# Cross-attention rows of a decoder layer: the maximum added in the visit of the scores, masked places written from a broadcast tile

## The chip, the cores and the metric

The kernel runs on one core of one Trainium2 chip. The metric is device time in microseconds (us) of one execution. Five engines work side by side, each through its own instructions in order: TensorE (PE; its weight loads are listed as PEld), VectorE (DVE), ScalarE (ACT), GpSimd (POOL) and SyncE (SP), which here issues nearly all DMAs. They wait for one another by semaphores. PE writes its products to PSUM, eight banks of 2 KB per partition; DVE and ACT read them there; GpSimd works on SBUF alone.

## The reference, cut to what matters

One decoder layer with pre-normalisation, for 128 sequences of 128 tokens and width 256, in f32, with 16 heads of 16:

```python
x = x + self_attention(layernorm(x))
x = x + cross_attention(layernorm(x), ctx, ctx, mask)
x = x + ffn(layernorm(x))        # 256 -> 1024, exact gelu, layernorm, -> 256, ternary weights

# inside the cross attention:
scores = einsum('bhqd,bhkd->bhqk', Q, K) / sqrt(16)
scores = where(mask == 0, 1e-09, scores)       # one mask for all sequences and heads
attn = softmax(scores)
```

A masked place is not left out of the softmax: its score is 1e-09, and it gets the weight exp(1e-09 - max).

## The kernel before, in words

**Groups, rows and streams.** The 128 sequences are 32 groups of 4 (`G`). A group's tokens are 512 columns. What a group needs is written as Python generators that yield between pieces: `n` (load x, normalise, transpose, self queries, keys and values), `k` (load the context, cross keys and values), `c` (self projection, normalise, cross queries), `f` (cross projection, normalise, FFN, store), and `A`, the attention itself, which runs over all groups. Three strings, START, ORDER and END, name the stream that takes the next step, letter by letter (line 860). They are the order of the program: nothing reorders it afterwards. ORDER is repeated 28 times, and each repeat carries one group of every stream. So every engine's instruction order is fixed by these strings, and a piece of PE work between two attention steps is what covers DVE's and ACT's share of an attention row.

**An attention row** is one sequence with 16 heads, 128 x 128 scores each. `attention()` (line 822) walks through rows, four self rows of one group and four cross rows of the group before. For a row `here` with its neighbours `following` and `before`, it takes these steps:

- `maxima(following)` (line 680): PE computes scores with queries on partitions into all four score banks (two tiles of two banks, `ps_s`). In a cross row, sixteen small matmuls (L689, `never`) first put -1e30 at masked places. DVE takes maxima with two reductions (L711), negated, into `negm`; in a cross row `least` keeps them below the masked score (L717).
- `outputs(before)` (line 797): PE multiplies weights with values (L806), ACT copies the result to `raw` (L809); the values carry a column of ones, so the sums of weights come along.
- `transposed_scores(here)` (line 752): PE computes scores again, with keys on partitions (L761), into the same four banks. In a self row the queries already hold the maximum, added by `q_max` (L733). In a cross row DVE then writes the constant 1e-09 to masked places, with a predicated copy (L771) whose source is one column, `masked_score`.
- `transposed_maxima(following)` (line 725): PE turns `negm` over (L728). In a cross row ACT and DVE split it into three bf16 parts (L743 to L749), `negm_t`.
- `weights(here)` (line 778): in a cross row sixteen bf16 matmuls (L785) add the parts to the scores, masked places too, and ACT takes the exponentials (L794), one instruction for each pair of banks.

Thus a cross row uses its score banks from the scores through masking, additions and exponentials, and PE visits them twice. In the strings a cross row takes five letters A and a self row four. The stationary operand of the additions is `add_max`, a bf16 tile of 4 x 128 columns with equal columns for each of the four:

```python
rows = ident_strips[:, :, n:12:4]
nc.vector.tensor_reduce(row_of[:, n : n + 1], rows, AX.XY, ALU.add)
nc.vector.tensor_copy(add_max[:, n], row_of[:, n : n + 1].to_broadcast([P, P]))
```

**Keys and raw outputs.** `keys_values` (line 349) keeps a unit's keys in one tile of 512 columns, in two versions by the parity of the head; each is written by one ACT instruction of 512 columns (L358) for each half of the width, and three such tiles exist. `outputs` fills a `raw` tile of 512 columns over four rows. After the fourth, `rearranged` (line 385) issues two DMAs for the sums (L390) and eight for the outputs (L396), SBUF to SBUF. `projected` (line 399) takes reciprocals (L402), stores them to DRAM (L405), loads them back spread over partitions as `factors` (L408), and GpSimd multiplies (L414) before the output projection (L336, `po`).

**Other rows that the steps below use.** `transposed` (line 290) normalises with DVE's statistics (L275, L276), GpSimd's rstd (L281, L282) and its subtraction and product (L286). `hidden` (line 434) and `second` (line 469) are the FFN: products `ph` (L443) with Gelu (L450), normalisation on DVE or GpSimd (L286), transposes `pg` (L477), a split in two parts on ACT (L486) and DVE (L488), and products `py` (L501). `split` (L431, L432) does the like for the FFN's input. ACT loads a table for Gelu (L438) and one for Exp (L452). Three banks (`ps_mm`) serve all products but the attention's, one bank (`ps_av`) serves outputs and turned maxima. The last group is finished by `finish_rows` (line 608) in pieces x, y and z.

Of the kernel before, what the change touches and what calls it, by code (L numbers as in the profile page):

```python
# [53 lines left out]
    "nnnnnnwnwnnnwnnnAnAAnnAwnAAnAnAnAAAAAnnAAknnwAnnnnwnccnkAnnAAnnAnAkAcccckcAAcAnAAkccAccccntAAkAAnkAn"  # L54
    "AnAAnAkckAnnAnAcAnAnAnntAnAAAckccAccckkAAknAkAnknAnckcnAcAActAAftkAAAncAcAAntAAAffffAffnAnfnAnnAAnAn"
    "kAffnAAkfcfAffkfAAfknncffAAffffAkkfAnfcAcnfAfAffAAccfAc"
)
ORDER = (
    "ncfAfffAAkkAccAAcfcAnnfAAAccAffAAnnkAAnnAnfAnkAAAfffAfffnAAkcnnAnnAnAfkfkcAffffffAAfffAfffAfccccfffA"
    "fkfkAAAncfAn"  # L60
)
END = (
    "cfAfAffAfAcAcffcAfAAckAAxcAkcfffAAfffAAkfAAAAAkffkAcfAcAfffffAffAffccfffAcckcfckfAffAfAkkAfcAcfAAffc"
    "cAcfcAfAfkAAffAkAkfkAAAAfAfAffffAAxxAffAxAfffAxfffyfAfffffyfxAyffffAfxyxxxzxyfxfffzffyxzzffxxxxyyzxx"
    "yyzzzyzzz"
# [4 lines left out]
def tile_decoder_layer(ctx: ExitStack, tc: tile.TileContext, a: dict, out: bass.AP):  # L70
# [118 lines left out]
    for stage in ("self", "cross"):  # L189
        negms[stage] = const.tile([P, S4, 8, 4], F32, name=f"negm_{stage}")  # L190
# [10 lines left out]
    add_max = const.tile([P, 4, P], BF16, name="add_max")  # L201
# [39 lines left out]
    def constants():  # L241
# [15 lines left out]
        for n in range(4):  # L257
            rows = ident_strips[:, :, n:12:4]
            nc.vector.tensor_reduce(row_of[:, n : n + 1], rows, AX.XY, ALU.add)
            nc.vector.tensor_copy(add_max[:, n], row_of[:, n : n + 1].to_broadcast([P, P]))  # L260
        for i in range(2):
            rows = ident_strips[:, :, 4 * (i + 1) : 12]
# [86 lines left out]
    def keys_values(w, src_t, unit):  # L349
# [3 lines left out]
        for o in range(CC):  # L353
            pk = yield from product_halves(w["k"], o, src_t, "pk")
            if o == 0:
                kt = unit["k"] = p_act.tile([P, CC, 2, T], F32, name="kt", tag="kt", bufs=3)
            for e in range(2):
                nc.scalar.activation(  # L358
                    kt[:, o, e],
                    pk,  # L360
                    AF.Identity,
                    bias=w["bk"][:, o, e : e + 1],
                    scale=parity[:, e : e + 1],
                )
# [20 lines left out]
    def rearranged(raw):  # L385


        sums = p_stat.tile([P, T // 8], F32, name="sums", tag="sums", bufs=2)
        for o in range(CC):
            nc.sync.dma_start(sums[o * 64 : (o + 1) * 64], raw[HD :: P // S4, 2 * o : 2 * o + 2])  # L390
        o_raw = p_act.tile([P, CC, T], F32, name="o_raw", tag="o_raw")
# [514 lines left out]
```

## Time and profile before

| what | value |
|---|---|
| three executions | 2736.03, 2736.43 and 2738.77 us, median 2736.43 |
| profiled execution | span 2733.8 us from first to last instruction; 2.6 us less than the median |
| distance of two repeats of ORDER | 82.87 us |
| busy in one repeat | PE 82.51, DVE 65.18, ACT 49.21, POOL 41.76 us |
| bytes moved | 130.28 MB, mean 48 GB/s |
| q1, the queue that SyncE feeds | 125.11 MB, 19.0% of 16 DMA engines |

The page's time of the profiled execution is its span. A row of its groups reads: line, engine, operation, output tile and input tiles, shapes and count, then busy us, mean ns of one, and the engine's idle time before such instructions with what ended it. In a timeline the columns are start us, duration us, engine, line and operation, tiles, count, and in brackets the idle time before it. Ends of matmuls are modelled, so a busy PE can hide small gaps.

### The profile page before, as it was taken

To read this page: it belongs to the slowest core of one execution; us is meant where nothing else is said; L and a number is where in the kernel's file an instruction comes from. 1 tells how busy PE (TensorE), PEld (TensorE's weight loads), DVE (VectorE), ACT (ScalarE), POOL (GpSimd) and SP (SyncE) were. 2 spreads that over 40 slices of the span, in tenths; PEclk is the share of its full clock that TensorE was granted. 3 is DMA by queue.
4 is the path that set the end of the run, shared out by engine and by line. 5 is a ranking of instruction groups with operands and counts; after the bars stand their busy time and mean duration, and the time that the engine had idled before them with its cause. 6 is when DMAs were issued, how large, how long until landed. Compare 5 with 4: busy or idle time off the path is not lost.

```text
span 2733.8 us, 77048 instructions
## 1 busy us (share of the span) xinstructions
PE 2676.2 (98%) x32845; PEld 1917.3 (70%) x32845; DVE 2118.7 (78%) x3916; ACT 1579.2 (58%) x2508; POOL 1337.1 (49%) x1425
## 2 busy tenths in 40 slices
PE   7999999999999999999999999999999999999998
PEld 4567777677777767776777776777777777777666
DVE  5677787777787777887777887777877778877777
ACT  3455666655665655665556666556656556665446
POOL 3344554544554554554445545445545445545443
PEclk9999999999999999999999999999999999999999
DMA  4121111221111221122211112211112211212210
GB/s 118 33 50 42 41 41 50 57 57 34 46 44 50 57 58 28 46 49 51 58 42 41 42 50 57 58 42 42 42 49 58 58 31 44 49 49 50 50 26 16
DMA packets 110093, 130.28 MB, mean 48 GB/s; under 512 B 32312, under 2 KB 69048, under 8 KB 109752
## 3 DMA queue, kind: packets, MB, share of 16 engines
q1 hardware_dynamic: 109464, 125.11, 19.0%
q8 instruction: 259, 4.24, 0.6%
q14 instruction: 82, 0.67, 0.1%
q10 hardware_dynamic: 288, 0.26, 0.0%
HBM read 71.38 MB, written 18.84 MB: 33 GB/s over the span
## 4 chain that ended last, share of the span: by engine, by line
PE 89%; DVE 7%; issue 2%; POOL 1%; ACT 1%; DMA 0%; ACTq 0%; DVEq 0%; SPq 0%; POOLq 0%
PE st L761 10%; PE av L806 9%; PE pq L324 9%; PE s L700 9%; PE ph L443 9%; PE py L501 8%; PE pk L324 8%; PE po L336 8%; PE pv L336 8%; PE pt L304 3%; PE pg L477 2%; PE s L689 2%; PE st L785 2%; DVE mx L711 1%; DVE g L488 1%
## 5 line engine op out<-in xcount | busy, mean ns | idle before, releaser
L711 DVE TENSOR_REDUCE mx<-s 128x8 f32<-128x1024 f32 x512 | 601.3, 1216 | 83.0 <-PE s L700 82.5
L794 ACT ACTIVATE w_t<-st 128x1024 f32<-128x1024 f32 x512 | 496.7, 1022 | 202.5 <-PE st L785 122.3
L281 POOL TENSOR_SCALAR rstd<-agg 128x4 f32<-128x4 f32 (+2 forms) x163 | 39.0, 239 | 965.5 <-DVE agg L276 965.5
L286 POOL TENSOR_SCALAR xn<-x,agg,rstd 128x256 f32<-128x256 f32 x378 | 458.4, 1226 | 9.9
L771 DVE COPY_PREDICATED_SCALAR st<-masked_t,masked_score 128x1024 f32 x256 | 316.1, 1280 | 68.1 <-PE st L761 68.1
L414 POOL TENSOR_TENSOR o_raw<-o_raw,factors 128x256 f32<-128x256 f32 x252 | 181.0, 745 | 382.9 <-DMA factors<-by_head 277.0
L809 ACT COPY raw<-av 128x512 f32<-128x512 f32 x256 | 151.0, 590 | 315.3 <-PE av L806 310.4
L486 ACT ACTIVATE g<-pg,ln_w 128x256 fp32r<-128x256 f32 (+1 forms) x520 | 205.8, 473 | 175.8 <-PE pg L477 163.6
L700 PE MATMUL s<-kt,qt 32*128 32x256 f32 x4096 | 298.8, 402 | 3.2 <-ACT w_t L794 2.2
L501 PE MATMUL py<-w_proj,g 128*128 128x256 f32 x2048 | 279.6, 289 | 1.3 <-DVE g L488 0.8
L806 PE MATMUL av<-w_t,v 128*32 128x128 f32 x8192 | 276.9, 276 | 0.5 <-DVE q_max L733 0.5
L806 PEld LDWEIGHTS av<-w_t,v 128*32 128x32 f32 x8192 | 209.0, 109 | 96.7 <-issue 80.0
L443 PE MATMUL ph<-w_fc,xn 128*128 128x512 f32 x1024 | 259.8, 404 | 4.2 <-ACT g L450 1.6
L501 PEld LDWEIGHTS py<-w_proj,g 128*128 128x128 f32 x2048 | 254.1, 189 | 13.2 <-issue 1.3
L286 POOL TENSOR_SCALAR g<-g,agg,rstd 128x1024 f32<-128x1024 f32 x63 | 241.1, 3828 | 6.6
L488 DVE SCALAR_TENSOR_TENSOR g<-pg,ln_w,g 128x256 fp32r<-128x256 f32 (+1 forms) x520 | 212.6, 469 | 30.3 <-ACT g L486 29.9
L700 PEld LDWEIGHTS s<-kt,qt 32*128 32x128 f32 x4096 | 187.8, 185 | 63.7 <-issue 40.2
L443 PEld LDWEIGHTS ph<-w_fc,xn 128*128 128x128 f32 x1024 | 184.8, 188 | 58.7 <-DVE xn L432 10.0
L761 PEld LDWEIGHTS st<-q_max,kt 32*128 32x128 f32 x4096 | 129.2, 186 | 61.1 <-DVE negm_self L722 42.5
L275 DVE BATCH_NORM_STATS2 stats<-g 128x6 f32<-128x512 f32 x256 | 160.9, 670 | 0.8 <-ACT g L450 0.8
L450 ACT ACTIVATE g<-ph 128x512 f32<-128x512 f32 x256 | 146.5, 599 | 25.3 <-PE ph L443 24.2
L761 PEld LDWEIGHTS st<-qt,kt 32*128 32x128 f32 x4096 | 128.1, 186 | 46.3 <-DVE mx L711 26.4
(130 smaller groups left out, 4612.8 us busy)
## 6 DMA issues: line engine op xcount, KB each, us to landing
o_raw<-raw SPq DMA_DIRECT2D x504, 64.0 KB
factors<-by_head SPq DMA_DIRECT2D x126, 256.0 KB
ctx_t<-in_ctx_t_dram SPq DMA_DIRECT2D x32, 512.0 KB
x<-in_x_dram SPq DMA_DIRECT2D x31, 512.0 KB
out_dram<-x SPq DMA_DIRECT2D x31, 512.0 KB
sums<-raw SPq DMA_DIRECT2D x126, 16.0 KB
by_head<-r SPq DMA_DIRECT2D x63, 32.0 KB
raw_w<-in_w_fc_t_dram SPq DMA_DIRECT2D x1, 1024.0 KB
```

Of the source, the lines that this page charges most:

```text
L286: engine.tensor_scalar(dst[:, j], src[:, j], agg[:, j, 0:1], rstd[:, j : j + 1], ALU.subtract, ALU.mult)
L324: nc.tensor.matmul(out, w[:, c, o * P : (o + 1) * P], src_t[:, c], start=(c == 0), stop=(c == CC - 1))
L336: nc.tensor.matmul(rows[:, j], src_t[:, c, (j0 + j) * P : (j0 + j + 1) * P], w[:, c], start=(c == 0), stop=(c == CC - 1),)
L443: nc.tensor.matmul(ph, xn_parts[i][:, c, (j0 + j - at) * P : (j0 + j - at + 1) * P], w_fc[:, c, n * 512 : (n + 1) * 512], start=((i, c) == ...
L488: nc.vector.scalar_tensor_tensor(parts[1][:, f0 + f, tok], pieces[:, f], scales[f], parts[0][:, f0 + f, tok].bitcast(F32), ALU.mult, ALU.s ...
L501: nc.tensor.matmul(rows[:, j], parts[i][:, f, j * P : (j + 1) * P], w_proj[:, f], start=((i, f) == terms[0]), stop=((i, f) == terms[-1]),)
L700: nc.tensor.matmul(s[r // 2][:, r % 2, 2 * o : 2 * o + 2], qt[strip, o, tok], kt[strip, o, :, tok], start=(stage == "self"), stop=True, sk ...
L711: nc.vector.tensor_reduce(mx[:, 2 * half : 2 * half + 2], s[half], AX.X, ALU.max, negate=True)
L761: nc.tensor.matmul(s[r // 2][:, r % 2, n], kt[strip, n // 2, n % 2, tok], added[strip, n // 2, n % 2] if stage == "self" else qt[strip, n ...
L771: nc.vector.copy_predicated(s[half].rearrange("p r n q -> p (r n) q"), masked_t[:, None, :].to_broadcast([P, 8, P]), masked_score[:, :, No ...
L794: nc.scalar.activation(w_t[:, 2 * half : 2 * half + 2], s[half], AF.Exp)
L806: nc.tensor.matmul(av[32 * r : 32 * r + 32, n], v[:, j, head : head + 32], w_t[:, r, n], start=True, stop=True)
```

## The change

- **Additions first.** In a cross row the additions of the maximum now stand ahead of the scores, in one visit of PE in `transposed_scores`. `weights` is gone, and the predicated copy and the exponential follow pair of banks by pair of banks.
- **Masked places** are written last, so their value is 1e-09 - max, and differs by query and head. ACT writes the turned maxima plus 1e-09 to `m_rows`; one DMA stores 16 rows of it in DRAM (`by_row`, 8 KB), another loads them on all 128 partitions (`masked_as`, 1 MB, a single buffer). The predicated copy reads this tile.
- **Order of steps.** `transposed_maxima` of a following cross row comes before `transposed_scores` of the present row, and the load of `masked_as` is issued after it. A cross row takes four letters A. START, ORDER and END are new strings: 179, 108 and 269 letters for 255, 112 and 209.
- **Weights of the additions**: `add_max` has one column for each of the four, read 128 times by a step of 0. `negm` of cross rows lays out its parts the other way round.
- **Half tiles.** Keys are two tiles of 256 columns (five in all, for three of 512), each written by twice as many ACT instructions of 256 columns. `raw` is a tile of two rows (three buffers), and ten DMAs follow each half. The reciprocals go to DRAM in two DMAs.

Line numbers of the changed kernel differ by a few from those above.

```diff
 ORDER = (
-    "ncfAfffAAkkAccAAcfcAnnfAAAccAffAAnnkAAnnAnfAnkAAAfffAfffnAAkcnnAnnAnAfkfkcAffffffAAfffAfffAfccccfffA"
-    "fkfkAAAncfAn"
+    "AfffAnkAnnAfnAcnnnnnAnffAnfAfAfnnnfcffAAfffkAffffkAccccfffkAffkAAfAcfffAfknfkAcAAfAfAAkncfAcfAccAAAn"
+    "cckAAffA"
 )
...
-    add_max = const.tile([P, 4, P], BF16, name="add_max")
+    add_max = const.tile([P, 4], BF16, name="add_max")
...
-                kt = unit["k"] = p_act.tile([P, CC, 2, T], F32, name="kt", tag="kt", bufs=3)
-            for e in range(2):
-                nc.scalar.activation(
-                    kt[:, o, e],
-                    pk,
-                    AF.Identity,
-                    bias=w["bk"][:, o, e : e + 1],
-                    scale=parity[:, e : e + 1],
-                )
+                kt = unit["k"] = [
+                    p_act.tile([P, CC, 2, T // 2], F32, name="kt", tag="kt", bufs=5) for _ in range(2)
+                ]
+            for half in range(2):
+                for e in range(2):
+                    nc.scalar.activation(
+                        kt[half][:, o, e],
+                        pk[:, half * T // 2 : (half + 1) * T // 2],
+                        AF.Identity,
+                        bias=w["bk"][:, o, e : e + 1],
+                        scale=parity[:, e : e + 1],
+                    )
...
-    def rearranged(raw):
+    def rearranged(raw, half, sums, o_raw):
...
         for o in range(CC):
-            nc.sync.dma_start(sums[o * 64 : (o + 1) * 64], raw[HD :: P // S4, 2 * o : 2 * o + 2])
+            at = half * 64 + o * 32
+            nc.sync.dma_start(sums[at : at + 32], raw[HD :: P // S4, 2 * o : 2 * o + 2])
...
-                dst = o_raw[s * 32 + e * HD : s * 32 + (e + 1) * HD]
+                dst = o_raw[s * 32 + e * HD : s * 32 + (e + 1) * HD, :, half * T // 2 : (half + 1) * T // 2]
                 nc.sync.dma_start(dst, pairs[s * 32 : s * 32 + HD, e])
...
-        nc.sync.dma_start(by_head.rearrange("o h (j t) -> (o h j) t", j=8), r)
+        for half in range(2):
+            dst = by_head[:, :, half * T // 2 : (half + 1) * T // 2].rearrange("o h (j t) -> (o h) j t", j=4)
+            nc.sync.dma_start(dst, r[half * 64 : (half + 1) * 64])
...
+        rows = p_att.tile([P, P], F32, name="m_rows", tag="m_rows", bufs=1)
+        nc.scalar.activation(rows, pn, AF.Identity, bias=masked_score)
+        by_row = p_dram.tile([H, P], F32, name="by_row", tag="by_row")
+        nc.sync.dma_start(by_row, rows[0::8])
         first = p_att.tile([P, P], BF16, name="first", tag="first", bufs=1)
...
+    def masked_scores(by_row):
+        masked = p_att.tile([P, H, P], F32, name="masked_as", tag="masked_as", bufs=1)
+        nc.sync.dma_start(masked, by_row[None].to_broadcast([P, H, P]))
+        return masked
...
         if stage == "cross":
+            negm_t, masked = added
             for n in range(4):
                 for r in range(S4):
                     strip = slice(r * 32, (r + 1) * 32)
                     nc.tensor.matmul(
                         s[r // 2][:, r % 2, n],
-                        add_max[strip, n],
-                        added[strip],
-                        start=False,
-                        stop=(n == 3),
+                        add_max[strip, n : n + 1].to_broadcast([32, P]),
+                        negm_t[strip],
+                        start=(n == 0),
+                        stop=False,
                         skip_group_check=True,
                     )
...
         for half in range(2):
+            if stage == "cross":
+                nc.vector.copy_predicated(
+                    s[half].rearrange("p r n q -> p (r n) q"),
+                    masked_t[:, None, :].to_broadcast([P, 8, P]),
+                    masked[:, 8 * half : 8 * half + 8],
+                )
             nc.scalar.activation(w_t[:, 2 * half : 2 * half + 2], s[half], AF.Exp)
...
     def attention():
-        w_t = added = None
+        w_t = added = following_added = None
...
+            early = following and following[0] == "cross"
             if following:
                 negm = maxima(*following)
                 yield
             if before:
                 outputs(*before, w_t)
                 yield
+            if early:
+                negm_t, by_row = transposed_maxima(*following, negm)
+                yield
             if here:
-                s = transposed_scores(*here, added)
-                if not cross:
-                    w_t = weights(here[0], s, None)
-                yield
-            added_here = added
-            if following:
-                added = transposed_maxima(*following, negm)
-                yield
-            if cross and here:
-                w_t = weights(here[0], s, added_here)
-                yield
+                w_t = transposed_scores(*here, added)
+            if early:
+                following_added = negm_t, masked_scores(by_row)
+            if here:
+                yield
+            if following and not early:
+                following_added = transposed_maxima(*following, negm)
+                yield
+            added = following_added
```

## The prediction

> **What bounds the kernel now.** I read the page's busy shares first, then three stretches of the span, then one repeat of the order, then the rows that the change touches. The page:
>
> ```profile
> span 2733.8 us, 77048 instructions
> PE 2676.2 (98%) x32845; PEld 1917.3 (70%) x32845; DVE 2118.7 (78%) x3916; ACT 1579.2 (58%) x2508; POOL 1337.1 (49%) x1425
> PEclk9999999999999999999999999999999999999999
> PE 89%; DVE 7%; issue 2%; POOL 1%; ACT 1%; DMA 0%; ACTq 0%; DVEq 0%; SPq 0%; POOLq 0%
> ```
>
> TensorE (PE) is busy 98% at a full clock, and the chain of waits is 89% its own work. Where the other 2% lies is told by the busy time in stretches (stretch, its length, then PE, weight loads, DVE, ACT, POOL):
>
> ```profile
> 0.00:166.00 166.00, 141.61 (x1613) 90.02 (x1613) 108.45 (x218) 67.23 (x95) 64.78 (x83) 0.99 0.27 70
> 166.00:2570.00 2404.00, 2392.79 (x29687) 1719.14 (x29676) 1887.56 (x3473) 1425.57 (x2260) 1208.02 (x1275) 1.00 0.20 47
> 2570.00:2733.80 163.80, 141.81 (x1562) 108.19 (x1560) 122.72 (x227) 86.44 (x153) 64.28 (x67) 0.98 0.11 28
> ```
>
> In the middle PE idles 2404.00 - 2392.79 = 11.2 us, in the first 166 us 24.4, in the last 164 us 22.0. The length of one repeat is the distance between two context loads in SyncE's timeline:
>
> ```profile
> 1345.36 0.55 SPq L102 DMA_DIRECT2D ctx_t<-in_ctx_t_dram  x1
> 1428.23 0.53 SPq L102 DMA_DIRECT2D ctx_t<-in_ctx_t_dram  x1
> ```
>
> 82.87 us, of which PE is busy 82.51. ORDER runs 28 times: 28 x 82.87 = 2320 us of the span. So a repeat can lose 0.36 us of visible idle and what hides in the modelled ends; it can grow by any wait of PE.
>
> **PE's own work.** Counted from the order in which each engine's instructions stand, the changed kernel gives PE the same matmuls: 4096 scores, 2048 maxima additions, 2048 for the masked rows, 256 transposes of maxima, and so on line by line. Only their places differ. Sixteen additions and sixteen scores now share one visit, so a repeat has four changes of work fewer of that kind, but its other pieces are cut differently: 79 visits in a repeat before, 79 after. An addition visit costs 58.5 us / 128 = 0.46 us and its shortest are 0.40 in the timeline, so 0.06 x 128 = 8 us is the most that sharing saves; the new cuts can take it back. I take 0, with -8 and +8 as ends.
>
> The additions' weights become one bf16 column read 128 times. Weight loads by shape:
>
> ```profile
> L761 PEld LDWEIGHTS st<-qt,kt 32*128 32x128 f32 x4096 | 128.1, 186 | 46.3 <-DVE mx L711 26.4 <-issue 7.6 <-DVE negm_cross L717 6.1
> L785 PEld LDWEIGHTS <-add_max 32*128 32x128 bf16 x2048 | 32.5, 92 | 42.8 <-issue 35.3
> ```
>
> If a repeated column loads like f32 (186 ns, not 92), a visit goes at the scores' pace, 16 x 1.10/32 = 0.55 us for 0.40: 0.15 x 128 = +19 us. Below nothing there is no reason: the bytes read are as many. I take 0, since the shape and type are those of the 92 ns row.
>
> The Trainium skill (TensorE: Matmul & The Clock Gate, Weight-path perf modes) says that fast loading needs 128 weights that are not FP32 and permits column steps of -1,023 to 1,024 elements. That includes 0 and makes this term 0; no run here shows it.
>
> **The scores' banks.** All four score banks go to one user at a time: maxima, then transposed scores, and so on. Rows that price a turn:
>
> ```profile
> L711 DVE TENSOR_REDUCE mx<-s 128x8 f32<-128x1024 f32 x512 | 601.3, 1216 | 83.0 <-PE s L700 82.5
> L794 ACT ACTIVATE w_t<-st 128x1024 f32<-128x1024 f32 x512 | 496.7, 1022 | 202.5 <-PE st L785 122.3
> L771 DVE COPY_PREDICATED_SCALAR st<-masked_t,masked_score 128x1024 f32 x256 | 316.1, 1280 | 68.1 <-PE st L761 68.1
> ```
>
> Before, a cross row needs 2 x 1.28 = 2.56 us of cover between scores and additions, and 2 x 1.02 = 2.04 between additions and the next maxima. After, masking and exponentials go half by half, in one piece: 1.28 + 1.28 + 1.02 + 0.2 of hand-overs = 3.8 us. With PE pieces priced from the chain of waits in order of time (query or key product 0.95 each, value product 0.49, hidden product 0.24, projection product 0.46, second FFN product 0.13, transpose 0.12), the new ORDER covers the four cross rows with 2 + 3 query and key products = 4.8; 8 hidden and 6 value products = 4.9; 8 projections, 8 transposes, one key product = 5.6; 32 FFN products, 9 transposes = 5.2. So 1.0 to 1.8 us are left for a late DVE or ACT. The reductions, 2 x 1.22 = 2.4, have 2.9 to 4.0 us between maxima and scores. This hides.
>
> The masked copy now reads a tensor and no column. Its nearest rows: the scalar form, 1.28, and a two-input DVE operation, 0.67 for 512 elements (L418), thus 1.35 for 1024. The dear end is two passes, about 2.35. I take 1.3. Below 1.28 there is no reason, the elements are the same.
>
> With two inputs in SBUF, the copy can meet GpSimd. A normalisation on DVE beside one on GpSimd shows what a meeting costs (start, us):
>
> ```profile
> 1363.38 3.79 POOL L286 TENSOR_SCALAR g<-g,agg,rstd 128x1024 f32<-128x1024 f32 x1
> 1365.04 0.80 DVE L286 TENSOR_SCALAR g<-g,agg,rstd 128x1024 f32<-128x1024 f32 x1
> 1370.87 3.79 POOL L286 TENSOR_SCALAR g<-g,agg,rstd 128x1024 f32<-128x1024 f32 x1
> 1371.33 1.28 DVE L286 TENSOR_SCALAR g<-g,agg,rstd 128x1024 f32<-128x1024 f32 x1
> ```
>
> The first DVE operation runs wholly inside GpSimd's 3.79 us and takes 0.80; the second, started 0.46 after GpSimd, takes 1.28. So a meeting costs 0 to 0.5 us, which the 1.0 us cover takes in.
>
> The Trainium skill says otherwise (SBUF — State Buffer, Who interferes with whom): a DVE instruction with two SBUF inputs and a GpSimd instruction that reads SBUF exclude each other for the whole instruction. By that rule a meeting with the 3.79 us row could cost up to 3.8 us, about 2 beyond the cover, once a repeat: some 60 us more. The rows above differ from it, and I go by them.
>
> **ACT.** Keys: 512 instructions of 256 columns for 256 of 512 at 0.78 (L358). Between half of that (0.39) and the 0.48 of L486's 256 columns, with 0.6 as dear end: at 0.48, 246 - 187 = +59 us. Rows of maxima: 128 x 0.27 (as L743) = +34 us. The hidden layer's Gelu is now cut by an Exp in 29 groups, which adds 58 table loads of 1.283 = +74 us. ACT goes to about 1746 us, 64%: it doesn't bind, but eight key instructions (3.8 us) now stand in front of the copies that feed the hidden products, and PE waits for those.
>
> **SyncE and DMA.** 504 moves of raw output become 1008, the sums 252, and each cross row adds two. An issue takes 0.59 (L396) or 0.65 (L408), in all some 34 us of a repeat: enough. But the queue is in order, and for cross rows 2 and 4 the ten moves stand ahead: 8 x 0.59 + 2 x 0.56 = 5.8, row store 0.45, its landing 1.9 (118.4 us over 63 waits of L408 for by_head), load issue 0.65, transfer. The page's queue took 19.0% of 16 engines for 125.11 MB, so 1.05 MB in 16 shares takes 0.19 x 2733.8 x 1.05/125.11 = 4.4 us. Together 13.2 us, against 17.0 and 17.7 us of PE work, summed by the same prices, from the end of the copied output to the end of the scores that need the tile. The load also waits until the row before has been masked, which with 11 to 15 us between rows leaves over 3 us, and factor loads queued behind it have 10 us of slack before their projection. I take 0; if a transfer takes over 8 us, this cover is gone.
>
> **Waits that are new, and the sum.** Walking one repeat by these durations, PE waits at two places: the second cross row's maxima have 1.8 us of projections as cover for the last self row's 1.94 us of exponentials, behind a 0.27 us copy (up to 0.7), and the hidden products wait for the key instructions above (0.1 to 0.5). Against this stand 0.36 us of idle and some of the switch costs of before. Net I take +0.3 a repeat, from -0.4 to +1.0: 28 x 0.3 = +8. In END two cross rows have their next maxima directly behind the scores, so that the whole 3.8 us shows; before, the like place showed 1.85:
>
> ```profile
> 2645.06 0.39 PE L689 MATMUL s<-never,ident_b 32*32 32x512 bf16 x2 [1.32 <-ACT w_t L794]
> 2645.97 0.43 PE L689 MATMUL s<-never,ident_b 32*32 32x512 bf16 x14 [0.53 <-ACT w_t L794]
> ```
>
> 2 x 1.95 = 3.9, and about 2 at two shorter gaps: +6. START: 0, with 8 either way (a third of its idle). Sum +14. The median, 2736.4, is 2.6 above the profiled span; I set that 2.6 as unchanged: **2750 us**, span about 2747.
>
> **Rivals.**
> 1. Not slower: the shared visits shed switch costs and the walk above overstates the waits. Idle in the middle goes (-11) and half of the 8 us is kept: 2736 - 11 - 4 = 2721, with START's ends 2712 to 2738. It decides if new waits stay under about 0.1 us a repeat. For: the covers are even, 4.8 to 5.6. Against: PE already idles only 0.36 us a repeat.
> 2. The repeated column loads slowly: 2750 + 19 = 2769.
> 3. The masked copy takes 2.35 us: the turn becomes 5.9 against covers of 4.8, 4.9, 5.6, 5.2, so 1.1 + 1.0 + 0.3 + 0.7 = 3.1 us in each of some 30 groups, 93 us: 2843.
> 4. The tile comes late: a transfer of 11 us makes the 13.2 us 19.8, and puts cross rows 2 and 4 back by 2 to 3 us, less the 1 us of cover; at 2 each 30 x 4 = 120, so 2870. Against: the 4.4 us above.
>
> **Chances.** "Same" is within 0.2%, 5.5 us, about what a measurement tells from no change. Forecast, 0.45 (its own range 2738 to 2768): slower 0.37, same 0.08. Rival 1, 0.32: faster 0.25, same 0.07. Rival 2, 0.09; rival 3, 0.08; rival 4, 0.06, all slower. Faster 0.25, same 0.15, slower 0.60. Leaving out rivals 3 and 4 and the lowest 0.05 of rival 1 gives 2718 to 2800.
>
> **What would show it.** Context loads 83.2 us apart (82.5 or less is rival 1; 86 or more is 3 or 4). A masked copy of about 1.3 us. Weight loads of the additions near 92 ns. No wait of DVE for the masked tile's DMA among the long waits. ACT near 1750 us, 189 table loads. Last maxima of END waiting 3 to 4 us for the exponentials. The prediction fails if DVE's masked copy is much dearer, if SyncE's queue holds the tile back, or if START moves by over 10 us.

## The result and the profile after

| | before | changed |
|---|---|---|
| median of four executions, us | 2737.32 | 2785.09 |
| lowest and highest | 2736.03 to 2738.77 | 2780.60 to 2790.52 |
| span of the profiled execution | 2733.8 | 2784.3 |
| one repeat of ORDER (mean of 28) | 82.81 | 83.96 |

The changed kernel takes 1.0178 times as long (95% interval 1.0164 to 1.0193). That is +48 us, where +14 was forecast. The page of the changed kernel, to be held against that of before:

```profile
span 2784.3 us, 79867 instructions
...
PE 2674.6 (96%) x32845; PEld 1915.9 (69%) x32845; DVE 2106.2 (76%) x3916; ACT 1756.6 (63%) x2950; POOL 1487.7 (53%) x1425
...
PEclk9999999999999999999999999999999999999989
...
PE 71%; DVE 10%; POOL 10%; ACT 7%; issue 1%; DMA 1%; SPq 0%; POOLq 0%; ACTq 0%; DVEq 0%
```

PE does the same busy time (2674.6 us; 2676.2 before), so by the page, whose matmul ends are modelled, the 50 us of span are idle time of PE. The chain that ended last went from 89% PE to 71%, and GpSimd (POOL) has 10% of it for 1%. GpSimd's busy time grew by 150.6 us though its 1425 instructions are the same: they got slower. The stretches, cut at the same maxima as before (columns as before):

```profile
0.00:168.60 168.60, 145.59 (x1609) 91.39 (x1609) 107.52 (x220) 72.76 (x117) 58.95 (x79) 0.94 0.31 94
168.60:2608.80 2440.20, 2384.55 (x29709) 1713.64 (x29700) 1876.11 (x3471) 1590.76 (x2666) 1353.53 (x1274) 1.00 0.31 97
2608.80:2784.30 175.50, 144.49 (x1557) 110.87 (x1544) 122.59 (x227) 93.05 (x167) 75.22 (x75) 0.93 0.22 74
```

The first stretch is 2.6 us longer than before, the middle 36 (2440.20 for 2404.00) with 55.7 us of idle PE instead of 11.2, the last 12 longer with a clock of 0.93. Cut where ORDER ends (2484.6 us before, 2519.5 after), the 50.5 us are START +2.6, the 28 repeats +32.3, END +15.6. Two context loads stand 83.91 us apart, between the 83.2 and the 86 that the prediction had set as marks:

```profile
1351.01 0.39 SPq L101 DMA_DIRECT2D ctx_t<-in_ctx_t_dram  x1
...
1434.92 0.39 SPq L101 DMA_DIRECT2D ctx_t<-in_ctx_t_dram  x1
```

What PE waits for, from the view of waits of that engine (us in total, times, longest; `pt` are the transposes, `pn` the turned maxima, `s` the scores for the maxima):

```profile
PE pt L304 <- POOL xn L286: 45.7, 70, 2.3
PE pn L730 <- DVE negm_cross L719: 21.9, 31, 2.9
PE s L691 <- ACT w_t L801: 11.4, 10, 3.9
```

Before, the first and the third were 4.0 and 2.6, and the second was not there. The first is transposes that wait for the normalised tile that GpSimd writes. Why GpSimd is late, one repeat's timelines tell: first GpSimd's, then DVE's, then PE's.

```profile
1359.07 1.12 POOL L281 TENSOR_SCALAR rstd<-agg 128x4 f32<-128x4 f32 x1 [8.41 <-DVE agg L276]
1360.28 1.85 POOL L282 TENSOR_TENSOR rstd<-rstd,minus_half 128x4 f32<-128x4 f32 x1
1362.24 4.83 POOL L286 TENSOR_SCALAR xn<-x,agg,rstd 128x256 f32<-128x256 f32 x4
```

```profile
1358.90 2.35 DVE L796 COPY_PREDICATED st<-masked_t,masked_as 128x1024 f32<-128x1024 int32 x2
```

```profile
1365.93 0.33 PE L304 MATMUL pt<-ident,xn 128*128 128x128 f32 x1 [0.31 <-POOL xn L286]
1367.13 0.77 PE L304 MATMUL pt<-ident,xn 128*128 128x128 f32 x5 [0.87 <-POOL xn L286]
```

DVE's two masked copies run from 1358.90 to 1361.25. GpSimd's addition of epsilon to four numbers starts 0.17 us into the first and ends with it (1.12 us; 0.246 at the most before). Its power function starts beside the second and takes 1.85. Together they are 1.7 us late (1.12 + 1.85 against 0.24 + 1.04), and PE idles 0.31 + 0.87 = 1.18 us. This happens in every repeat: 33.0 us of gaps at the transposes in the 28 repeats. The groups say how common the meeting is:

```profile
L281 POOL TENSOR_SCALAR rstd<-agg 128x4 f32<-128x4 f32 x95 | 51.3, 540 | 779.9 <-DVE agg L276 772.5 <-DVE xattn_bqs L206 7.4
...
L282 POOL TENSOR_TENSOR rstd<-rstd,minus_half 128x4 f32<-128x4 f32 x95 | 124.7, 1312 | 7.9
...
L796 DVE COPY_PREDICATED st<-masked_t,masked_as 128x1024 f32<-128x1024 int32 x256 | 319.7, 1294 | 6.6 <-PE st L785 6.6
...
L773 PEld LDWEIGHTS <-add_max 32*128 32x128 bf16 x2048 | 29.6, 93 | 63.8 <-issue 63.5
```

The mean of this form of L281 is 540 ns, and of all its 163 cases 62 start inside a copy and take 1.12 us. The copy itself (1.29 us in the mean) and the weight loads of the repeated column (93 ns) are as forecast.

The second wait stands at the turned maxima of the last cross row. Its chain in one repeat, first on DVE, then on PE:

```profile
1379.93 1.29 DVE L275 BATCH_NORM_STATS2 stats<-g 128x6 f32<-128x512 f32 x2 [0.85 <-ACT g L452]
...
1381.38 2.30 DVE L713 TENSOR_REDUCE mx<-s 128x8 f32<-128x1024 f32 x2
1383.71 0.25 DVE L719 TENSOR_SCALAR negm_cross<-mx,least 128x48 f32<-128x48 f32 x1
```

```profile
1384.11 0.30 PE L730 MATMUL pn<-ident,negm_cross 128*128 128x128 f32 x1 [0.56 <-DVE negm_cross L719]
```

DVE's statistics of the FFN wait 0.85 us for a Gelu, the reductions of the maxima stand behind them in DVE's order, and PE idles 0.56 us before it can turn the maxima: 15.8 us in the 28 repeats.

### The profile page after: what moved, and what is told of

It reads as the page before. It is cut to its first block, busy times and chain, and to the rows that moved or that the text cites. A ratio compares the mean times of both kernels' runs of the same rounds, so it can differ in the third digit from the quotient of the medians.

```text
span 2784.3 us, 79867 instructions
## 1 busy us (share of the span) xinstructions
PE 2674.6 (96%) x32845; PEld 1915.9 (69%) x32845; DVE 2106.2 (76%) x3916; ACT 1756.6 (63%) x2950; POOL 1487.7 (53%) x1425
## 4 chain that ended last, share of the span: by engine, by line
PE 71%; DVE 10%; POOL 10%; ACT 7%; issue 1%; DMA 1%; SPq 0%; POOLq 0%; ACTq 0%; DVEq 0%
PE py L503 9%; PE po L336 8%; PE st L785 8%; PE av L817 8%; PE s L702 8%; POOL xn L286 6%; PE pv L336 6%; PE pq L324 5%; PE ph L445 4%; PE pg L479 4%; PE pk L324 3%; PE pt L304 3%; DVE stats L275 3%; DVE mx L713 3%; POOL rstd L282 2%; ACT w_t L801 2%
## 5 line engine op out<-in xcount | busy, mean ns | idle before, releaser
L801 ACT ACTIVATE w_t<-st 128x1024 f32<-128x1024 f32 x512 | 507.6, 1023 | 189.5 <-DVE st L796 119.1
L281 POOL TENSOR_SCALAR rstd<-agg 128x4 f32<-128x4 f32 (+2 forms) x163 | 93.8, 575 | 994.9 <-DVE agg L276 987.6
L286 POOL TENSOR_SCALAR xn<-x,agg,rstd 128x256 f32<-128x256 f32 x378 | 458.7, 1226 | 9.9
L416 POOL TENSOR_TENSOR o_raw<-o_raw,factors 128x256 f32<-128x256 f32 x252 | 225.7, 923 | 247.0 <-DMA factors<-by_head 149.3
L796 DVE COPY_PREDICATED st<-masked_t,masked_as 128x1024 f32<-128x1024 int32 x256 | 319.7, 1294 | 6.6 <-PE st L785 6.6
L702 PE MATMUL s<-kt,qt 32*128 32x256 f32 x4096 | 304.5, 404 | 4.2 <-ACT w_t L801 4.2
L445 PE MATMUL ph<-w_fc,xn 128*128 128x512 f32 x1024 | 286.7, 416 | 2.8 <-DVE v L375 2.2
L503 PE MATMUL py<-w_proj,g 128*128 128x256 f32 x2048 | 268.9, 285 | 3.3 <-DVE x L512 1.8
L445 PEld LDWEIGHTS ph<-w_fc,xn 128*128 128x128 f32 x1024 | 181.0, 189 | 56.7 <-DVE v L375 10.7
L282 POOL TENSOR_TENSOR rstd<-rstd,minus_half 128x4 f32<-128x4 f32 (+2 forms) x163 | 197.8, 1214 | 13.6
L304 PE MATMUL pt<-ident,xn 128*128 128x128 f32 x760 | 128.7, 287 | 53.2 <-POOL xn L286 45.7
L735 DVE SCALAR_TENSOR_TENSOR q_max<-pn,max_rows,qt 128x256 f32<-128x256 f32 x256 | 111.0, 475 | 84.7 <-PE pn L730 84.7
```

The source lines that it names most:

```text
L282: nc.gpsimd.tensor_tensor(rstd, rstd, minus_half.to_broadcast([P, g]), ALU.pow)
L286: engine.tensor_scalar(dst[:, j], src[:, j], agg[:, j, 0:1], rstd[:, j : j + 1], ALU.subtract, ALU.mult)
L416: nc.gpsimd.tensor_tensor(o_raw[:, o, tok], o_raw[:, o, tok], factors[:, o, tok], ALU.mult)
L445: nc.tensor.matmul(ph, xn_parts[i][:, c, (j0 + j - at) * P : (j0 + j - at + 1) * P], w_fc[:, c, n * 512 : (n + 1) * 512], start=((i, c) == ...
L503: nc.tensor.matmul(rows[:, j], parts[i][:, f, j * P : (j + 1) * P], w_proj[:, f], start=((i, f) == terms[0]), stop=((i, f) == terms[-1]),)
L702: nc.tensor.matmul(s[r // 2][:, r % 2, 2 * o : 2 * o + 2], qt[strip, o, tok], kt[strip, o, :, k_tok], start=(stage == "self"), stop=True, ...
```

## The experiments

Twelve kernels were run. Theory P: the masked copy, since it reads a whole SBUF tile, and GpSimd exclude each other for whole instructions, and this is what the forecast lacks. Its rivals: the new order by itself (O), the doubled traffic (D), a masked tile that comes late (L). The median of before beside each run lay between 2736.2 and 2739.2 us; every ratio is to that, with its 95% interval.

### The column as source of the copy, and the tile without its traffic

```diff
# e1_column
-                    masked[:, 8 * half : 8 * half + 8],
+                    masked_score[:, :, None].to_broadcast([P, 8, P]),
...
# e2_fixed: masked_as a constant tile, m_rows, by_row and both DMAs gone
-        masked = p_att.tile([P, H, P], F32, name="masked_as", tag="masked_as", bufs=1)
-        nc.sync.dma_start(masked, by_row[None].to_broadcast([P, H, P]))
-        return masked
+        return masked_as
```

> The changed kernel, but the predicated copy reads the one column of the masked score, as in the kernel before; the row store, the 1 MB load and their tile stay and nothing reads the tile. Left out: masked places get 1e-09 instead of 1e-09 - max. Theory P (port): a predicated copy that reads a full SBUF tile keeps every GpSimd instruction that starts beside it waiting until the copy ends; that lengthened rstd (L281, 0.24 to 0.57 us in the mean), the power (L282) and the factors (L416, 0.75 to 0.92), and TensorE pays where a transpose waits for the normalised tile: 33 us in the steady part, some 7 at the two ends. P expects L281 back at 0.24, L416 at 0.74, the gaps between transposes gone, and 2785 - 40 = 2745 us (2738 to 2755). Theory O (order): the new order puts the FFN's normalisation too close to its transposes whatever the copy reads: the gaps stay, 2780 to 2788. Theory D (traffic): the second 130 MB of DMA slow everything a little: the traffic stays, so 2780 to 2788.

Measured: 2883.87 us, 1.0516 (1.0492 to 1.0541). All three theories are wrong on the time. On the rows P is right: L281 is back at 239 ns, the factors' product (L416) at 732 for 923, and in the repeats no gap is left at the transposes. Yet the kernel is 99 us slower than the changed one. The row of L281 in e1_column:

```profile
L281 POOL TENSOR_SCALAR rstd<-agg 128x4 f32<-128x4 f32 x95 | 22.8, 239 | 808.0 <-DVE agg L276 800.6 <-DVE xattn_bqs L206 7.4
```

DVE's, GpSimd's and PE's timelines of one repeat of e1_column:

```profile
1416.19 4.14 DVE L719 TENSOR_SCALAR negm_cross<-mx,least 128x48 f32<-128x48 f32 x1
```

```profile
1414.75 2.80 POOL L426 TENSOR_TENSOR x<-x,b_proj 128x256 f32<-128x256 f32 x4
1417.50 2.78 POOL L426 TENSOR_TENSOR x<-x,attn_bo 128x256 f32<-128x256 f32 x4
```

```profile
1416.84 1.13 PE L336 MATMUL pv<-attn_wv,xn_t 128*128 128x256 f32 x4
1420.97 2.08 PE L445 MATMUL ph<-w_fc,xn 128*128 128x512 f32 x4 [3.00 <-DVE xn L434]
```

A DVE instruction on 48 elements, 0.25 us otherwise, takes 4.14: it starts while GpSimd is in a chain of eight additions and ends when the last of them does (1420.28). GpSimd, no longer held, had reached these additions 1.7 us earlier than in the changed kernel, counted from the same maxima; there, negm_cross started 0.27 us ahead of them. In e1_column this happens 27 times, in all but one of the repeats. The split behind it (L434) is late and PE idles 3.00 us. The stretches show what that does to the clock (the 1.00, 0.54, 0.50 ahead of the last two columns):

```profile
1416.00:1418.00 2.00, 1.83 (x32) 1.11 (x20) 1.97 (x2) 2.00 (x5) 2.00 (x4) 1.00 0.41 143
...
1420.00:1422.00 2.00, 1.03 (x3) 0.83 (x4) 1.52 (x3) 0.00 (x0) 0.34 (x2) 0.54 0.51 195
...
1424.00:1426.00 2.00, 2.00 (x31) 1.35 (x33) 0.70 (x2) 1.02 (x4) 0.79 (x2) 0.50 0.02 4
```

Behind each of the 27 gaps of 3.0 us the granted clock is 0.50, for 3.4 us in 12 cases and 6.8 us in 15, as here. That is why the gap costs more than its own 3.0 us: a repeat of e1_column takes 87.77 us, 3.8 above the changed kernel's although 1.2 us of its waits are gone.

> The changed kernel, but the predicated copy reads a full tile that is written once at the start; m_rows, the row store and the 1 MB load are gone. Left out: masked places get 1e-09 instead of 1e-09 - max. Theory P: the copy still reads SBUF at the same size, so L281 stays near 0.57 us and the gaps between transposes stay; ACT loses 34 us of work that bound nothing: 2785 (2778 to 2788). Theory D: moved bytes fall from 266 to about 131 MB and the time falls with them, by 20 us or more. Theory L (the tile comes late): DVE no longer waits for a load, the scores' turn gets shorter, 10 us or more less.

Measured: 2834.03 us, 1.0353 (1.0335 to 1.0370). Halving the bytes (130.46 MB) doesn't help, which speaks against D and L, though a new meeting (below) hides what it may be worth; L281 still meets the copy (0.57 us in the mean), as P says. The 49 us that it is slower than the changed kernel were expected by none. Its rows show a new meeting: 28 of the masked copies take 3.2 us beside GpSimd's factor products, since those, too, have shifted. The copy of the values stands behind them on DVE, and PE now waits 37.2 us for it, in 28 cases.

### The copy's source changed in the kernel before

```diff
# e3_before_tensor, in the kernel before
-                    masked_score[:, :, None].to_broadcast([P, 8, P]),
+                    masked_as[:, None, :].to_broadcast([P, 8, P]),
```

> The kernel before, but its predicated copy reads a 128 x 128 SBUF tile, repeated for eight heads by a step of 0 and written once, in place of the column; the result is the same. Theory P: of GpSimd's instructions in the trace of before, 58 normalisations of 256 elements, 28 of 1024 and some 11 others start inside a copy, with 1.01, 0.54 and 0.7 us of it left; each now ends later by that much, GpSimd's busy time goes from 1337 to about 1420 us; one of the 256-element kind in each repeat may be paid by TensorE, 28 x 1.0 = 28 at most: 2737 to 2765, 2745 likeliest. Theory O: nothing is lost, 2735 to 2740, and GpSimd's rows stay as they were. Both: a copy of 1.28 to 1.30 us.

Measured: 2762.76 us, 1.0085 (1.0070 to 1.0100), in P's range; GpSimd busy 1456.1 for 1337.1 us. This is P alone: nothing else has changed, no traffic, no order, no half tile, and the copy takes 1.28 us as before. GpSimd's normalisations, from the groups:

```profile
L288 POOL TENSOR_SCALAR xn<-x,agg,rstd 128x256 f32<-128x256 f32 x378 | 514.5, 1376 | 9.9
```

1226 ns became 1376 in the mean, because 30 of them took 3.11 us each; PE's waits for them went from 4.0 to 27.5 us:

```profile
PE pt L306 <- POOL xn L288: 27.5, 33, 0.9
```

The trace of the kernel before already had a sign that GpSimd can be the one that is late. Four of its 63 normalisations of 1024 elements took 4.33 us instead of 3.79, and each of the four started 0.07 us behind one of DVE's (GpSimd's, then DVE's):

```profile
200.78 4.33 POOL L286 TENSOR_SCALAR g<-g,agg,rstd 128x1024 f32<-128x1024 f32 x1
```

```profile
200.72 0.81 DVE L286 TENSOR_SCALAR g<-g,agg,rstd 128x1024 f32<-128x1024 f32 x1 [0.63 <-POOL rstd L282]
```

### Undoing the meeting of e1_column

```diff
# e5_column_adds = e1_column, and in finish():
-        add_row(x, b_proj)
         yield
         gs = []
         for j0 in range(0, G, 2):
             gs.append((yield from hidden(xn_parts, j0)))
+            if j0 == 0:
+                add_row(x, b_proj)
```

> As e1_column (the copy reads one column; masked places get 1e-09 instead of 1e-09 - max), and GpSimd's eight additions of the FFN's bias (L426, x + b_proj) are issued after the first hidden layer, not before it. In e1_column GpSimd was early by the 1.7 us that the copy no longer held it, began those additions before DVE's negm_cross (L719), and held it for 4.14 us in 28 of 128 cases; PE idled 2.9 us a repeat and its clock fell to half for 6 us after. Theory P2 (the lock works both ways, and only meetings cost): without that meeting nothing of e1's loss is left and the gain of the column shows: gaps between transposes gone, 2785 - 40 = 2745 us (2735 to 2765, the additions may meet something in their new place). Theory O (the order needs the late GpSimd, or the column costs by itself): 2850 or more as in e1.

Measured: 2757.55 us, 1.0080 (1.0063 to 1.0097). With the additions elsewhere, 126 us of e1_column's time are gone, and it is 27.5 us below the changed kernel. P2 holds, O falls. From the starts of PE's pieces, the transposes take 4.63 us a repeat in the changed kernel and 3.02 here (2.83 in the kernel before): 1.6 x 28 = 45 us is what the copy's lock costs there; in e1_column, where the copy's source alone differs, they take 3.02 too. Not all of it shows in the time: a repeat is 0.95 us shorter, so PE's other pieces lose 0.67. Which wait that is was not tried; negm_cross now takes 1.4 us in 25 cases beside GpSimd's additions, and PE's waits for the split (L434), 6.9 us, are new.

### Moves in ORDER

```diff
# e6_swap:       "...nnnnnAnffAnfAf..."   -> "...nnnnnAnAffnfAf..."
# e4_later_turn: "...AAfffkAffffkAcccc..." -> "...AAfffkffAffkAcccc..."
# e7_turn_one:   "...AAfffkAffffkAcccc..." -> "...AAfffkfAfffkAcccc..."
# e11_cover:     "...AAfffkAffffkAcccc..." -> "...AAfffkcAffffkAccc..."
# e12_three:     e6_swap, e11_cover and the additions of e5_column_adds
```

> The changed kernel with the same result; in ORDER the FFN's two transposing steps come after the outputs of the row before instead of ahead of them (AnffA becomes AnAff), so the late normalised tile has 1.0 us more of PE work as cover. Theory P: of the 1.18 us a repeat that PE waits there, 1.0 goes: 28 x 1.0 = 28 us, 2757 us (2750 to 2765). Rival M (what is moved meets another lock or queue: the FFN's splits and hidden products come 1 us later, GpSimd's additions stand where they were): the wait moves to the hidden products, 2775 to 2790, or over 2800 if an idle time of about 3 us halves the clock again.

Measured: 2766.07 us, 1.0116 (1.0101 to 1.0132). GpSimd is held as before (L281 1.12 us in 61 cases), but the wait of the transposes falls from 45.7 to 15.0 us, and 10.1 us come back at the hidden products. 19 us less, 1 us above P's range: the lock costs what stands uncovered behind it.

The second wait (pn, 15.8 us in the repeats) resisted three attempts:

> The changed kernel, but in ORDER the transposed maxima of the last cross row come two hidden products later (AAfffkAffffkA becomes AAfffkffAffkA). Theory W: the early transposition of the maxima waits for the reductions, which stand behind the FFN's statistics on DVE; that costs TensorE 0.57 us a repeat behind one key product, 15.8 us in all, and two more hidden products (1 us) cover it: 2785 - 16 = 2769 us (2766 to 2775). Rival: the wait comes back at the scores or at the next maxima, since it is DVE and ACT that are late: 2780 to 2790.

Measured: 2917.96 us, 1.0650 (1.0634 to 1.0666), far outside both. The gap before the turn is gone, and another has come:

```profile
PE pg L479 <- DVE x L420: 82.0, 28, 2.9
```

The timelines give the chain: on ACT two Gelus and a table load (1.28 us) now precede the copies of the turned maxima; on DVE the steps L751 and L755 wait for those copies, and behind them in its queue stand statistics, masked copies and the residual additions (L420) which free the bank that pg needs. A wait of 2.9 us again, and behind each of the 28 again a clock of 0.50, for 3.4 us.

> The changed kernel with the same result; the transposed maxima of the last cross row come one hidden product later (fffkAffffkA becomes fffkfAfffkA), half of e4_later_turn's step. Theory Q (the order on ACT decides: in e4 two Gelus and a table load stood ahead of the copies of the turned maxima, DVE waited for those, and behind DVE's wait stood the copies, the residual addition and a PSUM bank): with one Gelu (0.6 us) ahead the chain is 0.6 us late instead of 3, the 0.57 us wait of the turn is covered: 2785 - 16 + 0 to 10 = 2769 to 2780. Rival: any later turn breaks the chain as in e4: 2850 or more.

Measured: 2818.47 us, 1.0302 (1.0287 to 1.0318): neither. With half the step the wait for L420 is 0.6 us, a fifth, and 19.9 us of waits of the hidden products for the Gelu come in (19.8 in e4_later_turn). The size of the effect follows the step, as theory Q has it, but even one piece more costs more than it covers.

> The changed kernel with the same result; in ORDER one step of the output projection (four po matmuls, 0.9 us, no work for ACT or DVE behind it) goes in front of the last cross row's transposed maxima (AAfffkAffffkAcccc becomes AAfffkcAffffkAccc). The turn stays where it is among ACT's and DVE's instructions, unlike in e4_later_turn and e7_turn_one. Theory W (the wait of 0.57 us a repeat behind the key product is only missing cover): 2785 - 16 = 2769 us (2764 to 2775), and the gap between pk and pn gone. Rival X (the reductions come late because DVE and ACT are late all along this stretch, so that the wait goes to the scores or the next maxima): 2780 to 2790.

Measured: 2823.97 us, 1.0312 (1.0298 to 1.0326). Here nothing moved on ACT before the turn, only a PE piece. PE's waits:

```profile
PE ph L445 <- ACT g L452: 26.1, 28, 1.2
PE po L336 <- issue: 20.9, 28, 0.8
```

The moved product has to wait itself, 0.74 us before its first matmul and the next hidden product 0.91, the latter for the Gelu. That rival X is right in kind (the wait goes elsewhere) and wrong in size is all this shows. That it is a product bank, three of which serve all pieces and which a Gelu must empty, is the likely reason; it was not tried apart.

> The changed kernel with the same result and three moves at once: e11_cover's step, e6_swap's, and the FFN's additions on GpSimd after the first hidden layer as in e5_column_adds. Theory W + P: 2766 (e6_swap) - 16 = 2750 us (2743 to 2758), still above the kernel before, since the copy's lock and the ends remain. Rival: the moved additions meet a DVE instruction in their new place, or the moves add up badly: 2765 or more.

Measured: 2809.30 us, 1.0266 (1.0252 to 1.0280), in the rival's range. The loss of e11_cover outweighs the gain of e6_swap (2785 + 39 - 19 = 2805), and the moved additions bring nothing more.

### The shared visit alone, and the change in the old order

```diff
# e8_shared_visit, in the kernel before: transposed_scores of a cross row
+                    nc.tensor.matmul(s[r // 2][:, r % 2, n], add_max[strip, n], added[strip],
+                                     start=(n == 0), stop=False, skip_group_check=True)
...
-                    start=(n == 0),
-                    stop=(stage == "self"),
+                    start=(stage == "self" and n == 0),
+                    stop=True,
# and weights() without its matmuls
```

> The kernel before with one part of the change alone: in a cross row the sixteen additions stand ahead of the scores in one visit, then the copy from the column, then the exponentials in their old step. Order, full tiles, weights of the additions as before; masked places get 1e-09 instead of 1e-09 - max. Theory V: the shared visit is shorter by itself, as the trace of the changed kernel says (additions 0.234 us a visit for 0.42, scores of a cross row 1.04 for 1.10): about 1.05 us a repeat, 28 x 1.05 = 29 us: 2737 - 29 = 2708 us (2700 to 2720). Theory Z, as the prediction took it: at most 8 us: 2730 to 2740.

Measured: 2700.91 us, 0.9870 (0.9856 to 0.9885). It is the fastest of all runs, 35 us below the kernel before, by a part that the forecast took at 0. That is in V's range. It is no replacement, as masked places get another value. One addition visit and what follows it on PE, in the kernel before and in e8_shared_visit:

```profile
1366.55 0.40 PE L785 MATMUL st<-negm_t,add_max 32*128 32x128 bf16 x16
1366.99 3.69 PE L336 MATMUL po<-attn_wo,o_raw 128*128 128x256 f32 x16
```

```profile
1358.08 0.40 PE L761 MATMUL st<-negm_t,add_max 32*128 32x128 bf16 x16
1358.31 1.11 PE L773 MATMUL st<-qt,kt 32*128 32x128 f32 x32
```

The durations, with their modelled ends, are 0.40 us in both; but the next piece starts 0.44 us after the visit's start before, and 0.23 us here. In the mean of the repeats it is 0.415 us before and 0.235 here, and a repeat takes 81.44 us for 82.81.

```diff
# e9_old_order = changed kernel with START, ORDER, END and the step order of before
# e10_old_column = e9_old_order with e1_column's line
```

> The changed kernel in the order of before: START, ORDER and END of before, the transposed maxima after the scores, the exponentials in a step of their own; with the additions ahead of the scores in one visit, the masked tile through DRAM, and half tiles, all as changed. The result is the same. Theory S (the change is a sum: shared visit -35 as e8_shared_visit, the copy's lock on GpSimd +25 as e3_before_tensor, half tiles and traffic 0 to 10 since nothing on the path waits for them): 2737 - 35 + 25 + 5 = 2732 us (2724 to 2740). Theory L (the masked tile comes late where nothing was arranged for it; DVE waits for the load): over 2750.

Measured: 2935.63 us, 1.0739 (1.0715 to 1.0762). L is right here, and the sum S fails by 200 us. From the waits of e9_old_order:

```profile
DVE st L796 <- DMA masked_as<-by_row: 146.0, 38, 7.1
```

> As e9_old_order, but the copy reads the one column, while row store and load stay; masked places get 1e-09 instead of 1e-09 - max. Theory S: the lock alone goes, 25 us (15 to 35) less than e9_old_order, and what is left above e8_shared_visit is the price of half tiles, ACT's 34 us of rows, and the second 130 MB: 0 to 10 us, so 2701 to 2711. Theory A (half tiles, key instructions on ACT or the traffic are dear): 2720 or more, and within 10 us of e9_old_order.

Measured: 2778.60 us, 1.0154 (1.0139 to 1.0168). S expected 2701 to 2711; A is over its 2720, but not within 10 us of e9_old_order. Without the lock and without anyone who needs the tile, 78 us remain above e8_shared_visit. PE's waits name a load that isn't the tile's:

```profile
PE pk L325 <- DMA ctx_t<-in_ctx_t_dram: 51.3, 25, 10.7
```

The row store, the tile's load and the doubled raw moves stand in SyncE's one queue, and the context load behind them is late: 51.3 us in 25 waits, one of them 10.7 us. These are PE's waits for the load; how the other 27 us divide between half tiles, ACT's rows and the rest of the traffic was not tried. In the changed kernel's order neither wait exists: DVE never waits for masked_as there, and the loads that PE needs come in time. So the new order does pay for the tile's path. It also brought the change's two costs: the turned maxima ahead of the scores, and GpSimd's small steps of rstd beside copies. (In the old order a copy from a tile meets the normalisations, as e3_before_tensor shows.)

## Why the prediction was wrong, step by step

Direction and range held (2718 to 2800); the size did not. That the time fell into the range is partly luck, since two larger errors cancel in part. The steps:

- **PE's own work, taken as 0 with -8 as end: wrong, a gain.** From the starts of PE's pieces in the 28 repeats, additions went from 1.66 to 0.94 us a repeat and the cross rows' scores from 4.43 to 4.18: 0.97 x 28 = -27 us; alone, in the old order, the shared visit gave -35 (e8_shared_visit). The step that failed priced the visit by its shortest cases in a timeline, whose modelled ends say 0.40 in both kernels.
- **The meeting with GpSimd, "0 to 0.5 us, which the 1.0 us cover takes in": the failed step.** Measured, one GpSimd instruction loses 0.8 to 1.0 us in the changed kernel's common meetings (1.9 in those of e3_before_tensor), 150 us in all by GpSimd's busy time, and the transposes pay 1.6 us a repeat, 45 us (e5_column_adds against the changed kernel); in the kernel before, the same copy costs 25 us (e3_before_tensor). The row that was read showed a normalisation with one tensor input on DVE beside one on GpSimd, another pair of forms; and it was read for DVE being late, while here GpSimd is. The four rows of 4.33 us in the same trace, where GpSimd is the late one, have no place in the prediction. The Trainium skill's rule (SBUF — State Buffer, Who interferes with whom), which the prediction weighed and set aside, was right that the two exclude each other. The 60 us that the prediction made of it are too much, but they were of the right size: 45 and 25 were measured, where it took 0.
- **Turn of the banks: "The reductions ... have 2.9 to 4.0 us between maxima and scores. This hides." Wrong at one place of four.** The turned maxima stand ahead of the scores now, and at the last cross row DVE's reductions stand behind statistics that wait for a Gelu. 0.56 us a repeat, 15.8 us. Three moves that were to cover it (e4, e7, e11) cost more than they covered; that no order can isn't shown.
- **The masked copy, 1.3 us, and the column's weight loads, 92 ns: right** (1.294 us in the mean; 93 ns). Rivals 2 and 3 fall.
- **ACT, 1746 us and 189 table loads, not binding: right** (1756.6; 189). The parts were off: 0.57 us a key instruction for 0.48, 0.37 a row of maxima for 0.27.
- **SyncE and the tile, 0: right for this order**, wrong to think it slack: in the old order PE waits 51.3 us for a context load behind the same transfers, without the lock (e10_old_column). Rival 4 falls for the changed kernel and holds for e9_old_order.
- **The places where PE would wait**, the second cross row's maxima and the hidden products, at +8: the place failed. The hidden products wait 2.2 us for the copied values, and the maxima's waits for exponentials (11.4 us) are nearly all at the ends.
- **START 0: right** (+2.6). **END +6: undersized**, +15.6. The predicted part held: PE's gaps before maxima that wait for exponentials are 9.7 us there for 2.4. What came besides is the transposes' wait (9.0 us for 1.4), the turned maxima's (3.8 us), and a granted clock of 0.95 for 0.99 in that part, some 10 us of slower running in 265. What each gives apart was not tried.

In the 28 repeats the terms are, in us a repeat: shared visits -0.97, transposes +1.81, key products with the wait behind them +0.65, hidden products cut into six visits for three +0.43, all other pieces -0.77; sum +1.15, the 32.3 us measured. The forecast for the repeats was +8, all of it from waits. So two errors of opposite sign, -27 us in the shared visits and about +51 us in the rest (+59 for +8), lie under it.

## What to carry to other kernels

Before a DVE instruction gets a second SBUF tensor, list which GpSimd instructions start beside it and who waits for them, and look for a row of that very pair of forms, both ways round. A small shift can create or dissolve a meeting that costs 100 us in 2800, so one part of a change should be priced in an order that it doesn't disturb as well as in its own. Price visits of a pipelined engine from start to start, not from modelled ends.

## What the runs showed of the hardware that was not expected

- **The hold is for whole instructions, and depends on the pair of forms.** Medians over the first six traces (before, changed, e1 to e4), in us, alone and when started beside a copy from a tile, or from a column:

| GpSimd instruction | alone | beside copy from tile | beside copy from column |
|---|---|---|---|
| + epsilon (rstd) | 0.24 | 1.12 | 0.24 |
| power (rstd), 2 numbers | 0.73 | 1.54 | 0.73 |
| power (rstd), 4 numbers | 1.04 | 1.85 | 1.04 |
| normalisation, 256 | 1.22 | 3.15 | 1.22 |
| normalisation, 1024 | 3.79 | 5.23 | 3.79 before, 4.26 in e1_column |

  The addition of epsilon ends with the copy that it meets. A normalisation loses 1.9 us where one copy takes 1.23: it starts in the first of two copies that follow each other and is held through the second. The 4.26 us are not explained; DVE's own normalisation also runs beside GpSimd's there.

- **The other way round it can last a chain.** negm_cross (0.25 us) beside GpSimd's two-input additions took 4.14 us, to the end of all eight. Beside GpSimd's normalisation of 3.79 us it took 0.25 (29 cases in e1_column). The Trainium skill's section above lets either side block the other for one instruction; a GpSimd normalisation that doesn't hold negm_cross, and a hold over a chain, are what these traces show beyond it.
- **A wait of 3 us costs more than 3 us.** After gaps of 3.0 us without a matmul the granted clock fell to 0.50 for 3.4 or 6.8 us (e1_column, 27 of 27), after 2.93 us for 3.4 us (e4_later_turn, 28 of 28); behind the 0.87 us gaps in the repeats of the changed kernel it stayed at 1.00. The Trainium skill (TensorE: Matmul & The Clock Gate, Part 1: The HAM clock gate) gives an idle window of about 3.4 us before half rate. The gaps measured here were shorter and enough.
